# A state-space, attention and expert kernel: four attention batches issued from one written table instead of three loops

## The chip, the cores and the metric

The kernel runs on one core of a Trainium2 chip. The metric is the device time of one execution in microseconds (us), as the median of several runs. TensorE (PE) multiplies matrices and transposes, VectorE (DVE) and ScalarE (ACT) work on SBUF and PSUM, GpSimd (POOL) on SBUF alone, and SyncE (SP) issues most DMAs. Each engine takes its instructions in the order in which they were issued to it.

## The reference

Two layers act on four images of 32 x 32 positions with 256 channels. The first is a convolution with a state-space scan. The second, cut to what matters here, works on the 1024 tokens of each image:

```python
def attn(x, W_qkv, b_qkv, W_out, b_out):          # x: tokens after a layer norm
    q, k, v = split(x @ W_qkv + b_qkv, 3)
    q = q - mean(q); k = k - mean(k)              # over channels
    q2 = q * q; k2 = k * k
    k2 = l2_normalize(k2 / (sum(k2) + 1e-7), axis=tokens)
    q2 = l2_normalize(q2 / (sum(q2) + 1e-7), axis=channels)
    kv = einsum("bnc,bnd->bcd", k2, v)
    t2 = einsum("bnc,bcd->bnd", q2, kv) / sqrt(1024)
    return (v + t2) @ W_out + b_out
...
t = t + attn(layer_norm(t), ...)
t = t + ffn(layer_norm(t), ...)   # 16 experts, top 2 of a softmax gate, silu(x w1) * (x w2) w3
```

## The kernel before

The scan's stage and the experts' stage are untouched by the change. Between them stands the stage in question: attention of four batches (`b` = 0 to 3), each held as eight tiles of 128 tokens in an SBUF tile `tbs[b]`, and the routing of tokens to experts. The whole stage is issued under a manual schedule: an engine runs what it is given in the order of the Python calls, and waits are added where an instruction needs another's result or a buffer that another still uses. A new tile in a buffer waits for every use of the old one.

The stage is made of small steps, each a function of a batch and a tile, half or part:

- `stat(b, i)`: layer-norm statistics of tile i on VectorE (L1263, L1264). For the last unit of the first layer, `last_turn(j)` transposes (copied by ScalarE), `last_product(j)` multiplies by the output weights (L1301) and `last_sum` adds the result to `tbs[3]`.
- `root` and `scaled`: square root on ScalarE, reciprocal on VectorE, and then the normed tiles `xh` on ScalarE. `turn_x(b, half)`: eight transposes of `xh` (L1280), copied out by L1281.
- `qk(b, i)`: a product of 512 columns (L1336), the bias on VectorE (L1341), two squares with sums on ScalarE into `sq`, and a bias added to `tbs[b]` on POOL (L1347). `fourth(b, i)`: the sum of fourth powers on ScalarE. `k2(b, half)`: a reciprocal on VectorE (`rk`), four scalings on ScalarE (L1368), squares and folds over the tiles on POOL (L1371 to L1384).
- `v_out(b, i)`: the product of v with W_out (L1459), added to `tbs[b]` by VectorE (L1463). `turn_q(b, half)`: eight transposes of `sq` (L1280). `norm_q`, `norm_k`: the two normalizations; `norm_k` needs `fold` of POOL. `kv(b, m)`: eight products summed in PSUM (L1411), `kv_out` copies them, `kv_w` multiplies by W_out (L1442) and scales on VectorE (L1446, L1449).
- `out(b, i)`: the product with `q2T` (L1469), added into `tbs[b]` by VectorE (L1473), and the statistics of the second norm.
- `expert_in(b, half)`: normed rows `xe` on ScalarE, written to DRAM (`xd`) by SP. `turn_e`, `gates`, `turn_g`: transposes, the gate's product (L1510) and its transposes back. `route(b)`: a generator of 22 pieces, nearly all on VectorE, that finds the two experts of a token and its place in their lists. It has a product `pc` (L1569, L1570), its weights are written to DRAM by SP, POOL and ScalarE code the places, two large comparisons `qh` (L1639) follow, and a product (L1648) is added to `found`.
- `sources` turns `found` into rows to gather, `fetch_rows` gathers them by POOL, `first_weights` and `next_weights` load the first experts' weights by SP. `next_weights` puts them where `tbs[0]`, `tbs[1]` and `tbs[2]` were.

PSUM is shared by tags: `pq` has three buffers (of qk and v_out), `pt` two (transposes), `po` two (out, kv_w, norm_k, gates, turn_g, the product of route), and `pk` one (kv and `pc`). `sq`, `k2`, `ksq`, `q2T`, `xe` and `xeT` have one buffer, `xh` and `xhT` two.

Before the change three loops set the order. A first one interleaves statistics of batch 0 with the last products of the first layer, a second one issues all of qk(0, i) with statistics of batch 1, and a third one goes over `o` = 0 to 3. It issues attention of batch `o` beside qk and k2 of batch `o + 1`, statistics of `o + 2`, and gates and routing of `o - 1`, whose pieces are taken by `on_with(steps, n)` at fixed places.

Of the kernel before, what the change touches and what calls it, by code (L numbers as in the profile page):

```python
# [33 lines left out]
def conv_ssm_attn_moe_kernel(ctx: ExitStack, tc: tile.TileContext, a: dict, out: bass.AP):  # L34
# [1628 lines left out]
                break  # L1663


    for i in range(NT):
# [1 line left out]
        if i % 2 == 1:
            last_turn(i // 2)
        if i % 2 == 0 and i > 0:  # L1670
            last_product(i // 2 - 1)
        if i % HT == HT - 1:
            root(batch[0], "ln2", i + 1 - HT, i + 1)
            scaled(0, i + 1 - HT, i + 1)
    turn_x(0, 0)
    last_product(TPB - 1)
    turn_x(0, 1)
    for i in range(NT):
        qk(0, i)
        if i > 0:  # L1680
            fourth(0, i - 1)
        if i == HT:
            k2(0, 0)
        stat(batch[1], "ln2", tbs[1], i)
        if i % HT == HT - 1:
            root(batch[1], "ln2", i + 1 - HT, i + 1)
            scaled(1, i + 1 - HT, i + 1)
    fourth(0, NT - 1)
    k2(0, 1)
# [102 lines left out]
    for o in range(NB):
        n = o + 1 if o + 1 < NB else None
        z = o - 1 if o > 0 else None
        s = o + 2 if o + 2 < NB else None

        def first_part(i):
            if n is not None:
                qk(n, i)
                if i > 0:  # L1800
                    fourth(n, i - 1)

        def look_ahead(lo, hi):
            if s is not None:
                for i in range(lo, hi):
                    stat(batch[s], "ln2", tbs[s], i)

        def scale_ahead():
            if s is not None:
                root(batch[s], "ln2", 0, NT)  # L1810
                scaled(s, 0, NT)

        def turn_next(half):
            if n is not None:
                turn_x(n, half)
# [12 lines left out]
        if z is not None:
            turn_e(z, 0)
        norm_q(o)  # L1830
        if z is not None:
            root(batch[z], "ln3", HT, NT)
            expert_in(z, 1)
        turn_next(1)
        first_part(1)
        on_with(steps, 2 * pace)
        look_ahead(0, 4)
        v_out(o, 2)
        if z is not None:
            gates(z, 0)  # L1840
            turn_e(z, 1)
        else:
            for j in range(TPB):
                stat(last, "ln1", ysb, j, TPB)
            root(last, "ln1", 0, TPB)
        kv(o, 0)
        on_with(steps, 40)
        look_ahead(4, 8)
        if z is not None:
            gates(z, 1)  # L1850
        first_part(2)
        if z is not None:
            turn_g(z)
            steps = route(z)
        else:
            for j in range(TPB):
                last_sum(j)
            constants(True)
        kv(o, 1)
        on_with(steps, 2 * pace)  # L1860
        kv_out(o)
        scale_ahead()
        v_out(o, 3)
        on_with(steps, 2 * pace)
        norm_k(o)
        first_part(3)
        on_with(steps, 2 * pace)
        kv_w(o)
        if n is None:
            first_weights("w2")  # L1870
        v_out(o, 4)
        on_with(steps, 1 * pace)
        first_part(4)
        on_with(steps, 1 * pace)
        if n is not None:
            k2(n, 0)
        out(o, 0)
        on_with(steps, 1 * pace)
        out(o, 1)
        v_out(o, 5)  # L1880
        first_part(5)
        out(o, 2)
        on_with(steps, 1 * pace)
        out(o, 3)
        root(batch[o], "ln3", 0, HT)
        v_out(o, 6)
        on_with(steps, 1 * pace)
        first_part(6)
        expert_in(o, 0)
        if z is None:  # L1890
            constants(False)
        out(o, 4)
        on_with(steps, 1 * pace)
        first_part(7)
        v_out(o, 7)
        if n is not None:
            fourth(n, NT - 1)
            k2(n, 1)
        out(o, 5)
        on_with(steps, 1 * pace)  # L1900
        out(o, 6)
        on_with(steps, 1 * pace)
        if n is None:
            on_with(steps, 40)
            sources(0, SOON, found[:, 0, :SOON], found[:, 1, :SOON])
            given_rows.update(range(SOON))
            for key in soon[:3]:
                fetch_rows(key)
        out(o, 7)
        nc.scalar.dma_start(out=rows(of, o), in_=tbs[o])  # L1910
        if n is None:
            root(batch[o], "ln3", HT, NT)
            expert_in(o, 1)
            choices(0, SOON)
# [330 lines left out]
```

## Time and profile before

| | |
|---|---|
| median of 3 runs | 3376.29 us (3375.55 to 3376.74) |
| the profiled execution | 3389.96 us |
| its span, first to last instruction | 3387.8 us |
| PE busy over the span | 94% |
| DVE, ACT and POOL busy | 85%, 80% and 80% |
| first tile of `tbs[0]` landed | 2704.06 us |
| first product of kv(0, 0) | 2744.9 us |
| first product of kv(3, 0) | 2903.6 us |
| first expert product (L2008) | 2951.1 us |

Times in the profile are microseconds from the first instruction. A line of the timeline gives start, length, engine, line of the kernel, operation, the tile written and those read, shapes and the number of merged instructions. A last bracket gives the idle time of the engine ahead of it and what ended it. A matmul's record includes its way through the array, so starts are compared and not lengths. PEld is the loading of weights into TensorE, and a name with q is an engine's queue of instructions that are not counted as busy. PEclk is the granted clock of TensorE as a share of the full one.

### The profile page before, as it was taken

How to read it: one execution, taken by the hardware profiler on the slowest of the kernel's cores; microseconds unless marked ns; L12 is line 12 of the kernel's file. 1: busy time of each engine (PE TensorE's matmuls, PEld its weight loads, DVE VectorE, ACT ScalarE, POOL GpSimd, SP SyncE). 2: the span in 40 equal slices, each digit the busy share in tenths (PEclk: the TensorE clock that was granted, in tenths of full speed). 3: DMA queues.
4: the chain of work that ended last, by engine and by line, in shares of the span. 5: the costliest groups of instructions: out<-in, count | busy, mean ns of one | idle time of the engine just before them, and what ended most of it. 6: DMA issues, size and time to landing. Idle time of an engine off the chain costs nothing. (4 is left out here: it accounts for less than half of the span.)

```text
span 3387.8 us, 62750 instructions
## 1 busy us (share of the span) xinstructions
PE 3172.2 (94%) x23407; PEld 2753.3 (81%) x23407; DVE 2886.9 (85%) x3435; ACT 2717.3 (80%) x4621; POOL 2718.4 (80%) x1215
## 2 busy tenths in 40 slices
PE   7899999999999999999999999989999889789998
PEld 4588888988898888888988988768778756589998
DVE  4699999999999999999999999999999867652222
ACT  1699999999999999999999999899999754322221
POOL 0488998999999989999998999899999842234443
PEclk9999999999999999999999999999999999999999
DMA  3552224224333332253334223423222210467785
GB/s 105 150 68 63 68 66 69 71 71 62 67 78 69 68 72 76 62 63 74 73 73 68 71 64 60 71 54 68 60 62 67 80 48 29 156 186 231 214 245 149
DMA packets 423835, 300.76 MB, mean 89 GB/s; under 512 B 225073, under 2 KB 329393, under 8 KB 423522
## 3 DMA queue, kind: packets, MB, share of 16 engines
q1 hardware_dynamic: 397202, 274.25, 32.9%
q0 software_dynamic: 14016, 18.05, 2.8%
q10 hardware_dynamic: 12304, 4.37, 0.5%
q8 instruction: 187, 3.06, 0.4%
q14 instruction: 126, 1.03, 0.1%
HBM read 262.34 MB, written 34.87 MB: 88 GB/s over the span
## 5 line engine op out<-in xcount | busy, mean ns | idle before, releaser
L961 POOL TENSOR_TENSOR h<-h,cb_n 128x2048 f32<-128x2048 f32 x512 | 2154.9, 4226 | 142.6 <-DVE h L954 89.9
L928 ACT ACTIVATE da<-dt,l_conv_a_log_sb 128x512 f32<-128x512 f32 x2048 | 1438.3, 714 | 32.4 <-DVE h L954 31.3
L908 ACT ACTIVATE bx<-dtxT,proj 128x512 f32<-128x512 f32 x1748 | 1246.9, 714 | 29.9 <-DVE dtxT L600 16.4
L975 PE MATMUL y<-ident,h 128*128 128x128 f32 x8192 | 1236.5, 274 | 8.9 <-POOL h L961 5.8
L954 DVE TENSOR_TENSOR_SCAN h<-da,last,ps 128x512 f32<-128x512 f32 x1024 | 1217.9, 1262 | 7.0 <-PE ps L940 1.8
L954 DVE TENSOR_TENSOR_SCAN h<-da,ps 128x512 f32<-128x512 f32 x1024 | 1169.8, 1201 | 41.8 <-DMA last<-h 16.8
L940 PE MATMUL ps<-ident,bx 128*128 128x128 f32 x6992 | 1119.0, 276 | 41.7 <-DVE h L954 29.4
L975 PEld LDWEIGHTS y<-ident,h 128*128 128x128 f32 x8192 | 979.0, 141 | 99.9 <-issue 20.6
L940 PEld LDWEIGHTS ps<-ident,bx 128*128 128x128 f32 x6992 | 819.7, 142 | 101.8 <-DVE h L954 81.1
L2015 DVE TENSOR_TENSOR hT<-s,p 128x256 f32<-128x256 f32 x146 | 61.4, 421 | 281.0 <-ACT s L2014 281.0
L940 PE MATMUL ps<-ident,bxp 128*128 128x128 f32 x800 | 237.6, 297 | 58.9 <-DVE h L954 46.0
L2033 POOL DMA_INDIRECT out_dram<-yb,src x73 | 116.0, 1589 | 212.3 <-DVE yb L2030 82.2
L2014 ACT ACTIVATE s<-p 128x256 f32<-128x256 f32 x146 | 56.1, 384 | 265.4 <-PE p L2008 262.6
L413 PE MATMUL bg<-pad,dgc 128*128 128x256 f32 x864 | 258.2, 380 | 0.4 <-DMA dgc<-diags 0.4
L940 PEld LDWEIGHTS ps<-ident,bxp 128*128 128x128 f32 x800 | 112.3, 140 | 142.0 <-DVE h L954 89.2
L919 POOL TENSOR_SCALAR bxp<-dtxT,proj 128x512 f32<-128x512 f32 x200 | 147.0, 735 | 59.5 <-DVE dtxT L600 59.5
L935 PE MATMUL ps<-dgb,dtxT 128*128 128x128 f32 x800 | 170.3, 295 | 22.5 <-DMA dgb<-diag_b 9.7
L2008 PE MATMUL p<-xT,w 128*128 128x128 f32 x1408 | 171.7, 275 | 2.2 <-ACT xT L1988 2.2
L2008 PEld LDWEIGHTS p<-xT,w 128*128 128x128 f32 x1408 | 167.4, 192 | 5.0 <-ACT xT L1988 2.9
L935 PEld LDWEIGHTS ps<-dgb,dtxT 128*128 128x128 f32 x800 | 120.5, 190 | 49.2 <-DVE h L954 36.2
L413 PEld LDWEIGHTS bg<-pad,dgc 128*128 128x128 f32 x864 | 130.5, 191 | 0.7 <-DMA dgc<-diags 0.7
L2008 PE MATMUL p<-xT,m 128*128 128x128 f32 x928 | 115.4, 278 | 0.0
(341 smaller groups left out, 2681.6 us busy)
## 6 DMA issues: line engine op xcount, KB each, us to landing
cb_n<-cd SPq DMA_DIRECT2D x512, 256.0 KB, 3.3
m<-in_L_ffn_w_dram SPq DMA_DIRECT2D x87, 512.0 KB, 5.6
w<-in_L_ffn_w_dram SPq DMA_DIRECT2D x60, 512.0 KB, 6.9
dgc<-diags SPq DMA_DIRECT2D x84, 192.0 KB, 3.1
diag_b<-zero SPq DMA_DIRECT2D x2, 4096.0 KB
dgb<-diag_b SPq DMA_DIRECT2D x100, 64.0 KB, 3.2
last<-h SPq DMA_DIRECT2D x256, 2.0 KB, 3.1
xd<-xe SPq DMA_DIRECT2D x8, 512.0 KB, 3.5
```

Of the source, the lines that this page charges most:

```text
L413: nc.tensor.matmul(made["bg"].rearrange("p (h w) -> p h w", w=WW)[:, blk(c, deep), :], made["dgc", m * 3 + i][:, j, :], pads[m][:, at : at ...
L908: nc.scalar.activation(t, made["dtxT", u][:, j, :], AF.Copy, scale=made["proj", u][:, j, R + n : R + n + 1])
L919: nc.gpsimd.tensor_scalar(t, made["dtxT", u][:, 0, :], made["proj", u][:, 0, R + n : R + n + 1], 1.0, ALU.mult, ALU.mult,)
L928: nc.scalar.activation(t, made["dt", u][:, m, :], AF.Exp, scale=A[:, m, n : n + 1])
L935: nc.tensor.matmul(t[:, blk(j, P)], made["dtxT", steps[s][0]][:, j, blk(m, P)], made["dgb", s], start=True, stop=True,)
L940: nc.tensor.transpose(t[:, blk(j, P)], made["bx", s, j][:, blk(m, P)], ident)
L954: nc.vector.tensor_tensor_scan(h[:, m, 1:], made.pop(("da", s, m)), made.pop(("dbx", s, m)), 0.0 if seg == 0 else last[b][:, n, m : m + 1] ...
L961: nc.gpsimd.tensor_tensor(h[:, :, :BANK], h[:, :, 1:], over_middle(made["c", s], DK), ALU.mult)
L975: nc.tensor.matmul(made["y", u][j][:, blk(m, P)], made["h", s][:, m, blk(j, P)], ident, is_transpose=True, start=n == 0 and m == 0, stop=n ...
L2008: nc.tensor.matmul(p12[:, j, s, :], w_of(w, key)[:, ck, blk(h + j, P)], on_b["xT", key][:, ck, :], start=(ck == 0), stop=(ck == CK - 1),)
L2015: nc.vector.tensor_tensor(on_b["hT", key][:, h : h + 2, :], s, p12[:, :, 1, :], ALU.mult)
L2033: s = nc.gpsimd.indirect_dma_start(of[:, :], bass.IndirectOffsetOnAxis(src[:, c : c + 1], 0), yb, None, bounds_check=NB * L - 1, oob_is_er ...
```

## The change

The three loops are replaced by one tuple of steps, `ORDER`, and a dictionary that maps the short names to the same functions. The tuple has 332 entries, 69 of which (`rs`) issue one piece of a batch's route; `tg` issues the first piece too, and entries beyond the 22nd piece do nothing. Each step is there as often as before. Tiles of a batch no longer come in ascending order, and steps of up to three batches are mixed. The copy of `tbs[b]` to the output is `wr`, `first_weights` is `fw` and `next_weights` is `nw`.

```diff
-    for i in range(NT):
-        stat(batch[0], "ln2", tbs[0], i)
...
-    steps = iter(())
-    for o in range(NB):
...
-        pace = 2 if n is None else 1
-        turn_next(0)
-        if o == 3:
-            first_weights("w1")
-            first_weights("w3")
-            next_weights()
-        v_out(o, 0)
-        turn_q(o, 0)
-        v_out(o, 1)
-        turn_q(o, 1)
-        first_part(0)
...
+    def rows_in(b, half):
+        if half:
+            root(batch[b], "ln3", HT, NT)
+        expert_in(b, half)
+
+    def scale_rows(b, half):
+        lo, hi = (0, NT) if half == 2 else (half * HT, half * HT + HT)
+        root(batch[b], "ln2", lo, hi)
+        scaled(b, lo, hi)
+
...
+    STEPS = {
+        "st": lambda b, i: stat(batch[b], "ln2", tbs[b], i),
+        "sc": scale_rows, "lt": last_turn, "lp": last_product, "ll": last_stats,
+        "ls": last_sums, "co": lambda first: constants(bool(first)), "tx": turn_x, "qk": qk,
+        "f4": fourth, "k2": k2, "vo": v_out, "tq": turn_q, "nq": norm_q, "kv": kv,
+        "ko": kv_out, "nk": norm_k, "kw": kv_w, "ou": out,
+        "r3": lambda b: root(batch[b], "ln3", 0, HT), "ei": rows_in, "te": turn_e,
+        "ga": gates, "tg": begin_route, "rs": lambda b: next(routes[b], None),
+        "fw": first_weights, "nw": next_weights, "so": first_lists, "wr": put_rows_out,
+        "ch": lambda: choices(0, SOON),
+    }
+    ORDER = (
+        ('st', 0, 0), ('st', 0, 6), ('lt', 0), ('lt', 1), ('st', 0, 5), ('st', 0, 2), ('lp', 0),
+        ('lt', 2), ('st', 0, 1), ('st', 0, 3), ('sc', 0, 0), ('st', 0, 4), ('st', 0, 7),
+        ('st', 1, 0), ('st', 1, 1), ('lp', 1), ('st', 1, 4), ('lt', 3), ('lp', 2), ('tx', 0, 0),
+        ('lp', 3), ('sc', 0, 1), ('qk', 0, 0), ('st', 1, 2), ('tx', 0, 1), ('st', 1, 3),
+        ('sc', 1, 0), ('qk', 0, 2), ('st', 1, 5), ('qk', 0, 5), ('qk', 0, 1), ('qk', 0, 3),
+        ('f4', 0, 5), ('f4', 0, 0), ('st', 1, 6), ('qk', 0, 4), ('st', 1, 7), ('vo', 0, 0),
+        ('f4', 0, 2), ('f4', 0, 4), ('vo', 0, 4), ('k2', 0, 0), ('qk', 0, 6), ('tx', 1, 0),
+        ('sc', 1, 1), ('f4', 0, 1), ('qk', 0, 7), ('vo', 0, 1), ('f4', 0, 7), ('tq', 0, 0),
+        ('f4', 0, 3), ('st', 2, 0), ('f4', 0, 6), ('k2', 0, 1), ('st', 2, 5), ('qk', 1, 0),
+        ('st', 2, 1), ('st', 2, 7), ('qk', 1, 1), ('tq', 0, 1), ('qk', 1, 2), ('f4', 1, 2),
+        ('vo', 0, 2), ('st', 2, 2), ('ll',), ('tx', 1, 1), ('f4', 1, 0), ('kv', 0, 0),
+        ('vo', 0, 7), ('st', 2, 6), ('qk', 1, 3), ('qk', 1, 4), ('vo', 0, 5), ('st', 2, 3),
+        ('nq', 0), ('st', 2, 4), ('qk', 1, 5), ('kv', 0, 1), ('ls',), ('ko', 0), ('nk', 0),
+        ('k2', 1, 0), ('kw', 0), ('co', 1), ('vo', 1, 1), ('sc', 2, 2), ('vo', 0, 6),
+        ('ou', 0, 0), ('ou', 0, 1), ('vo', 0, 3), ('f4', 1, 1), ('ou', 0, 2), ('tx', 2, 0),
+        ('qk', 1, 6), ('ou', 0, 3), ('f4', 1, 4), ('ou', 0, 6), ('vo', 1, 0), ('r3', 0),
+        ('ei', 0, 0), ('ou', 0, 4), ('f4', 1, 5), ('qk', 1, 7), ('st', 3, 0), ('f4', 1, 6),
+        ('ou', 0, 7), ('k2', 1, 1), ('st', 3, 5), ('tq', 1, 0), ('ou', 0, 5), ('kv', 1, 0),
+        ('f4', 1, 3), ('tq', 1, 1), ('wr', 0), ('f4', 1, 7), ('nq', 1), ('ei', 0, 1),
+        ('qk', 2, 0), ('tx', 2, 1), ('vo', 1, 2), ('te', 0, 0), ('qk', 2, 1), ('st', 3, 1),
+        ('te', 0, 1), ('st', 3, 2), ('f4', 2, 0), ('co', 0), ('st', 3, 6), ('ga', 0, 0),
+        ('ga', 0, 1), ('st', 3, 4), ('vo', 1, 3), ('nk', 1), ('tg', 0), ('st', 3, 7), ('rs', 0),
+        ('qk', 2, 2), ('kv', 1, 1), ('rs', 0), ('st', 3, 3), ('rs', 0), ('ko', 1), ('sc', 3, 2),
+        ('rs', 0), ('vo', 1, 6), ('qk', 2, 3), ('f4', 2, 2), ('rs', 0), ('rs', 0), ('kw', 1),
+        ('qk', 2, 4), ('f4', 2, 1), ('vo', 1, 4), ('rs', 0), ('ou', 1, 0), ('k2', 2, 0),
+        ('rs', 0), ('f4', 2, 3), ('ou', 1, 2), ('qk', 2, 6), ('rs', 0), ('rs', 0), ('rs', 0),
+        ('ou', 1, 3), ('ou', 1, 4), ('vo', 2, 1), ('qk', 2, 5), ('ou', 1, 1), ('qk', 2, 7),
+        ('vo', 1, 7), ('r3', 1), ('ei', 1, 0), ('k2', 2, 1), ('vo', 1, 5), ('f4', 2, 5),
+        ('tx', 3, 0), ('rs', 0), ('ou', 1, 5), ('ou', 1, 7), ('rs', 0), ('vo', 2, 0), ('rs', 0),
+        ('f4', 2, 4), ('vo', 2, 2), ('f4', 2, 7), ('rs', 0), ('te', 1, 0), ('kv', 2, 0),
+        ('tq', 2, 0), ('rs', 0), ('ou', 1, 6), ('f4', 2, 6), ('qk', 3, 0), ('qk', 3, 1),
+        ('tq', 2, 1), ('ei', 1, 1), ('vo', 2, 7), ('qk', 3, 2), ('ga', 1, 0), ('te', 1, 1),
+        ('rs', 0), ('rs', 0), ('rs', 0), ('rs', 0), ('rs', 0), ('ga', 1, 1), ('tx', 3, 1),
+        ('tg', 1), ('vo', 2, 4), ('rs', 1), ('rs', 1), ('rs', 0), ('rs', 1), ('wr', 1),
+        ('kv', 2, 1), ('f4', 3, 0), ('rs', 1), ('ko', 2), ('nq', 2), ('nk', 2), ('rs', 1),
+        ('qk', 3, 5), ('rs', 1), ('f4', 3, 1), ('rs', 1), ('kw', 2), ('qk', 3, 3), ('f4', 3, 3),
+        ('ou', 2, 0), ('vo', 2, 3), ('rs', 1), ('ou', 2, 4), ('qk', 3, 4), ('rs', 1),
+        ('ou', 2, 1), ('k2', 3, 0), ('f4', 3, 4), ('ou', 2, 3), ('ou', 2, 2), ('rs', 1),
+        ('r3', 2), ('qk', 3, 7), ('rs', 1), ('rs', 0), ('ei', 2, 0), ('vo', 2, 5), ('qk', 3, 6),
+        ('rs', 1), ('ou', 2, 7), ('vo', 2, 6), ('ou', 2, 5), ('te', 2, 0), ('ou', 2, 6),
+        ('f4', 3, 7), ('tq', 3, 0), ('ei', 2, 1), ('ga', 2, 0), ('rs', 1), ('vo', 3, 1),
+        ('tq', 3, 1), ('f4', 3, 6), ('fw', 'w3'), ('rs', 1), ('vo', 3, 0), ('te', 2, 1),
+        ('f4', 3, 2), ('k2', 3, 1), ('rs', 1), ('f4', 3, 5), ('rs', 1), ('rs', 1), ('vo', 3, 2),
+        ('nq', 3), ('rs', 1), ('ga', 2, 1), ('kv', 3, 0), ('tg', 2), ('rs', 1), ('rs', 2),
+        ('rs', 2), ('rs', 2), ('rs', 2), ('kv', 3, 1), ('nw',), ('ko', 3), ('wr', 2), ('rs', 2),
+        ('rs', 2), ('rs', 2), ('rs', 2), ('nk', 3), ('fw', 'w2'), ('vo', 3, 4), ('rs', 2),
+        ('rs', 2), ('kw', 3), ('vo', 3, 3), ('rs', 2), ('rs', 2), ('rs', 2), ('ou', 3, 0),
+        ('rs', 2), ('rs', 1), ('rs', 1), ('rs', 2), ('rs', 2), ('ou', 3, 1), ('ou', 3, 3),
+        ('rs', 2), ('ou', 3, 2), ('rs', 2), ('r3', 3), ('vo', 3, 5), ('rs', 2), ('ei', 3, 0),
+        ('ou', 3, 4), ('vo', 3, 6), ('rs', 2), ('rs', 2), ('rs', 1), ('so',), ('vo', 3, 7),
+        ('ou', 3, 6), ('fw', 'w1'), ('rs', 2), ('rs', 1), ('ou', 3, 5), ('ou', 3, 7), ('wr', 3),
+        ('ei', 3, 1), ('rs', 2), ('ch',),
+    )
+    for name, *at in ORDER:
+        STEPS[name](*at)
```

More of the change, by code (lines that the diff above doesn't have):

```diff
@@ L1663, in on_with @@
                 break
-    for i in range(NT):
-        stat(batch[0], "ln2", tbs[0], i)
[L1668 to L1689, printed above, removed]
     late = ex
@@ L1789, in fetch_rows @@
         on_b["xb", key] = t
-    steps = iter(())
-    for o in range(NB):
[L1793 to L1815, printed above, removed]
-        pace = 2 if n is None else 1
-        turn_next(0)
-        if o == 3:
-            first_weights("w1")
-            first_weights("w3")
-            next_weights()
-        v_out(o, 0)
-        turn_q(o, 0)
-        v_out(o, 1)
-        turn_q(o, 1)
-        first_part(0)
[L1828 to L1914, printed above, removed]
@@ new lines, in rows_in, with begin_route, last_stats @@
+    def rows_in(b, half):
[6 more added lines that the diff above has]
+        scaled(b, lo, hi)
+    routes = {}
+    def begin_route(b):
+        turn_g(b)
+        routes[b] = route(b)
+        next(routes[b])
+    def last_stats():
+        for j in range(TPB):
+            stat(last, "ln1", ysb, j, TPB)
+        root(last, "ln1", 0, TPB)
@@ new lines, in last_sums, with first_lists, put_rows_out @@
+    def last_sums():
+        for j in range(TPB):
+            last_sum(j)
+    def first_lists():
+        for b in routes:
+            for _ in routes[b]:
+                pass
+        sources(0, SOON, found[:, 0, :SOON], found[:, 1, :SOON])
+        given_rows.update(range(SOON))
+        for key in soon[:3]:
+            fetch_rows(key)
+    def put_rows_out(b):
+        nc.scalar.dma_start(out=rows(of, b), in_=tbs[b])
+    STEPS = {
[9 more added lines that the diff above has]
+    }
```

## The prediction

> **What bounds the kernel now.** I first read the windows of 20 us, to find the stage that the table orders. It begins when the last scan products leave TensorE, at 2698 us, and ends with the first expert matmul at 2951 us. The windows show which engine could be the limit:
>
> ```profile
> core 0: us, PE busy (x) PEld busy (x) DVE busy (x) ACT busy (x) POOL busy (x), PEclk, DMA share, GB/s
> 2720.00:2740.00 20.00, 16.09 (x56) 9.66 (x55) 12.89 (x34) 16.09 (x62) 8.59 (x8) 0.91 0.00 1
> ...
> 2800.00:2820.00 20.00, 19.37 (x79) 12.80 (x78) 11.38 (x39) 12.12 (x35) 0.00 (x0) 1.00 0.00 1
> 2820.00:2840.00 20.00, 15.45 (x60) 11.07 (x59) 17.35 (x46) 8.67 (x31) 10.74 (x9) 0.91 0.13 36
> ...
> 2920.00:2940.00 20.00, 16.80 (x71) 13.44 (x70) 16.46 (x45) 3.49 (x7) 1.47 (x1) 0.75 0.14 32
> ```
>
> No engine is full throughout. TensorE is near it at 2800 to 2820 us, VectorE at 2820 to 2840 us, and in the last row neither is, at a granted clock of 0.75. So order can matter. Next I read the timeline of TensorE, which shows where its time goes and what each idle stretch waited for (the last bracket):
>
> ```profile
> 2730.51 1.03 PE L1459 MATMUL pv<-wvs,xhT 128*128 128x256 f32 x4
> 2735.45 1.97 PE L1280 MATMUL ps_t<-ident,sq 128*128 128x128 f32 x8 [3.91 <-DVE xhT L1281]
> ...
> 2828.76 1.89 PE L1469 MATMUL po<-kvw,q2T 128*128 128x256 f32 x8
> 2833.82 1.59 PE L1469 MATMUL po<-kvw,q2T 128*128 128x256 f32 x4 [3.16 <-DVE tb L1473]
> ...
> 2868.71 1.89 PE L1442 MATMUL pkw<-wvs,kvT 128*128 128x256 f32 x8
> ...
> 2919.34 0.46 PE L1569 MATMUL pc<-hot,every_t 128*128 128x128 f32 x2 [3.29 <-DVE both L1572]
> 2919.64 0.59 PE L1570 MATMUL pc<-hot,before_t 128*128 128x128 f32 x2
> 2920.03 3.41 PE L1442 MATMUL pkw<-wvs,kvT 128*128 128x256 f32 x8
> ```
>
> Starts to starts on this timeline give the price of each step at full clock: qk 1.71 us (four records), vo and ou 0.86, kv 3.45, kw 1.73, lp 1.73, ga 1.75, tx, tq, te and nk about 0.87, tg 0.6. Times their counts, and with route's three products, they make 191 us. From 2699.4 us to the last `out` at 2940.9 us pass 241.5 us, so some 50 us are lost. About 38 are the bracketed gaps; the rest is slow matmul after a gap: the same eight pkw took 3.41 us behind a gap of 3.29, and 1.89 without one. Cut at the starts of kv(b,0), the losses are: up to kv(0,0) at 2744.9, 45.5 us for 33.5 of work, 12.0 lost; to kv(1,0) at 2796.0, 51.1 for 43.9, 7.2; to kv(2,0) at 2853.1, 57.1 for 46.7, 10.4; to kv(3,0) at 2903.6, 50.4 for 42.3, 8.1; to the last `out`, 37.4 for 25.0, 12.4.
>
> **The change part by part.** No instruction is added or removed: the steps are the same, and route's 22 pieces of each batch are all issued before first_lists. So only gaps can go or come. Behind the last `out` the order is unchanged (root, expert_in, turn_e, gates, then the first rows); those 10.2 us stay, and I price the experts' stage at nothing, if weights and rows are there in time (below).
>
> *Up to kv(0,0).* Both halves of tb0 are issued together; the first landed at 2704.06, and at 350 GB/s, which the DMA moved there, 512 KB more take 1.5 us. stat(0,6) now stands second and waits for that, so scaled(0,0) comes 2 us later. But in the old order the third last_turn's copy stood on ScalarE behind the four xh, and TensorE got to turn_x(0,0) at 2711.9 only. Now copies 0 to 2 precede the xh, and TensorE does its lp without holes: turn_x at 2709.5, qk(0,0) at 2712.9, turn_x(0,1) done at 2715.5, with 12.1 us of its work behind it. Before, it had 10.4 at 2715.9. That is 2.1 us. Then the gap of 3.91: ScalarE was busy from 2718.5 to 2737.7 with squares, xh of batch 1 and k2, and TensorE had run out. Now vo(0,0), vo(0,4), vo(0,1), tq(0,0) and qk(1,0) stand there, 5.2 us. The gap goes, and the slow matmuls behind it (ps_t 1.97 where 1.04 is usual, pv 1.80 for 1.03). 3.9 + 1.7 = 5.6. Together **7.7 us**. What is late next is ScalarE on sq(1,0): `sq` has one buffer, and tq(0,1) that frees it stands behind qk(1,1). It waits some 2 us, with k2(0,1) already done, and TensorE holds other work. If not covered, half of the 5.6 comes back.
>
> *kv(0,0) to kv(1,0).* Gaps of 1.63 (pkn behind the last sums), 1.38 (pkw) and some of 0.5. In the new order nk(0) alone lies between kv(0,1) and kw(0), where vo and qk stood, so kv_out (0.69 us) shows for 0.2; but vo(1,1) and vo(0,6) cover the two kvw. Then 13.7 us of TensorE against 14.9 of VectorE up to kv(1,0). I leave 3.7 of the 7.2 lost: **3.5 us** gained (bounds 0 and 5).
>
> *kv(1,0) to kv(3,0).* Of 18.5 lost, the worst places are runs of `out` at the end of a batch. VectorE needs 1.06 us for one (0.48 + 0.43 + 0.18, part of it overlapped), TensorE 0.86, and into that run fell the pieces of route and k2's rk, which waited 1.57 for squares just issued. Now vo(1,7), vo(1,5), turn_x(3,0) and later te(1,0) and kv(2,0) lie among them, and k2(3,1) follows its last qk by 20 steps. New waits: the evictions of tq(1,0) and tq(2,0) write the one q2T, and must wait for out(0,5) and out(1,6), which stand behind them on TensorE; sq(3,0) waits on ScalarE for tq(2,1), with gates' copy queued behind; route(0)'s five last pieces come in a row, so its product waits for two qh. 9 of the gaps can go (2833 with its slow matmuls 5, and 2890, 2896 for 4), the four waits cost 0 to 2.5 each, and I take 5 for all: **4 us** gained (bounds -1 and 9).
>
> *kv(3,0) to the last `out`.* gates(2,1), a qh and the product of route(1) leave the stretch between kv(3,0) and pc: 15.8 us for 11.7 of TensorE become about 11.5 for 9.2, 4 less. From pc on VectorE sets the pace, 24.1 us then and, with the same steps, now. Against it: `pf` of route(1) is taken 25 steps before it is used and holds one of two `po` buffers over nk(3), kw(3) and out(3,0), 1 us (0 to 3); fold(3) needs 8.4 us of POOL behind k2(3,1) and nk(3) comes 11 us of work later, 1 us (0 to 3). The third is VectorE against POOL. In POOL's timeline:
>
> ```profile
> 2835.59 1.89 POOL L1371 TENSOR_TENSOR ksq<-k 128x1024 f32<-128x1024 f32 x1 [8.45 <-ACT k L1368]
> ```
>
> VectorE's timeline around it, with the same operation twice:
>
> ```profile
> 2834.36 0.36 DVE L1604 TENSOR_TENSOR pick<-hot_all,run 128x128 f32<-128x128 f32 x1
> ...
> 2836.03 1.70 DVE L1604 TENSOR_TENSOR pick<-hot_all,run 128x128 f32<-128x128 f32 x1
> ```
>
> The same pick took 0.36 us alone and 1.70 when it began inside ksq, ending 0.25 us after it. The new order puts route(1)'s two qh (1.19 to 2.38 us) and route(2)'s first pieces beside the fold of k2(3,1), where POOL had been idle from 2905 to 2928. Two qh at 1.2 more and three picks or the like at 0 to 1.34 are 2.4 to 6.4; I take 4, near the middle; as such pieces were caught elsewhere before, at half that, 2 remain. The Trainium skill (SBUF — State Buffer, "Who interferes with whom") has the rule: a VectorE instruction with two SBUF inputs and a POOL instruction that reads SBUF exclude each other for a whole instruction. The trace agrees: the pick ended just after ksq. By the rule alone, an estimate with seven small ones each held for half of a 1.27 us fold would be 6.8 us where I took 4, and the forecast 3 us less gain.
>
> Sum here **0 us** (4 - 1 - 1 - 2; bounds -8 and 4).
>
> *The queue of SP.* next_weights now stands ahead of the copy out of tb2, whose place its third load takes:
>
> ```profile
> 2889.01 1.49 SPq L1773 DMA_DIRECT2D w<-in_L_ffn_w_dram  x2
> 2890.55 14.33 SPq L1753 DMA_DIRECT2D m<-in_L_ffn_w_dram  x6
> 2904.92 0.51 SPq L1494 DMA_DIRECT2D xd<-xe  x1
> ```
>
> SP held there for 14.33 us, 9.3 of them for such a copy, with xe's write queued behind. Now w2, route(2)'s weights and xe of batch 3 are behind it. It is free some 16 us after kv(3,1), 11 us behind pc, and the rows are gathered 22 us behind pc. w1, issued last, lands (6.9 us) 5 us before the first expert matmul. Cost nothing; without that cover, a us for each us.
>
> The sum: 7.7 + 3.5 + 4 + 0 = 15.2 us. The profiled execution took 3389.96 us (span 3387.8), 0.4% over the median of 3376.29; on the median the forecast is 3361, in a profile about 3375.
>
> **The rivals.**
> *Slower: steps ahead of what frees their buffer.* Five places (tq(1,0), tq(2,0), qk(3,0), pf, fold(3)) are priced small above. If each opens a TensorE gap like the 3.16, with 1.9 of slow matmuls behind it, they cost 25.5 us instead of 7, and the 15.2 become 3 lost; with POOL's collisions at their bound, 4.4 more, 3384. It decides from four such gaps. For it: gaps of 3 us did come from one late VectorE instruction. Against: in each place TensorE has 1 to 4 us of other work. Chance 0.2.
> *Only the beginning gains.* VectorE is busy 16 to 17 of 20 us in late windows, and `po` has two buffers whatever the order. The later gaps would move and not close: 8 us, 3368. The Trainium skill (Perfetto Trace Analysis, "Optimization Strategy") reads the same gap, repeated, as too few buffers, which speaks against any order; the trace shows 11 waits of po on L1473, but not evenly spaced. Chance 0.15.
> *Nearly full TensorE.* If only 20 of 50 us stay, 3346. For it, 2744 to 2828 ran with 7 lost of 84. Chance 0.12.
> *Given back.* Weights or rows come late and the experts begin when they did: 3376. Chance 0.06.
>
> **How the numbers follow.** The forecast has 0.47, by itself 3352 to 3370. A measurement of this kernel can tell about 0.2%, 6.8 us. The main case, the full one and half of the second are faster by more: 0.67. The other half and the last are within: 0.13. Slower 0.20. The range reaches from 3345, the full case, to 3382, which leaves out the worst half of the slower rival.
>
> **What would show it.** In the changed profile: the kv(0,0) products (L1411) 5 us earlier; no gap of 3 us before it; L1569 of batch 2 some 12 us after the last kv(3,0) began; a span from L1469's last to L2008's first of 10 us. I am wrong if TensorE gaps behind L1281 or L1473 add up to as much as before, or if L2008 waits for w or xb.

## The result, and the profile after

| | before | after |
|---|---|---|
| median | 3375.92 us (3375.08 to 3376.74, 4 runs) | 3352.47 us (3347.83 to 3355.56, 4 runs) |
| profiled execution | 3389.96 us, span 3387.8 | 3350.39 us, span 3348.6 |
| the stage, first last_turn to first expert product | 251.8 us | 226.6 us |
| experts' stage | 436.7 us | 438.7 us |

The kernel became faster by 23.45 us: the ratio is 0.9929 (95% interval 0.9916 to 0.9941). The two profiled executions differ by more, 39.6 us, because the scan's stage, with the same instructions in both, ended 16.1 us earlier in one than in the other (first last_turn at 2699.4 and 2683.3). So everything below is counted from the start of the stage. There 25.2 us were gained, and the experts gave back 2.0.

The windows of the changed kernel, cut at the starts of kv(b,0) and at the last `out`:

```profile
core 0: us, PE busy (x) PEld busy (x) DVE busy (x) ACT busy (x) POOL busy (x), PEclk, DMA share, GB/s
2682.50:2723.80 41.30, 37.66 (x157) 24.23 (x158) 26.39 (x74) 28.81 (x97) 13.79 (x15) 1.00 0.42 132
2723.80:2755.90 32.10, 32.10 (x143) 24.66 (x142) 26.53 (x77) 15.13 (x55) 18.87 (x28) 1.00 0.03 10
2755.90:2808.45 52.55, 49.52 (x214) 34.04 (x212) 41.49 (x120) 29.93 (x91) 19.37 (x19) 0.97 0.14 45
2808.45:2865.60 57.15, 56.11 (x259) 36.92 (x257) 49.84 (x126) 30.56 (x92) 19.46 (x19) 1.00 0.17 50
2865.60:2901.20 35.60, 27.72 (x145) 22.62 (x144) 32.17 (x86) 8.53 (x18) 12.14 (x9) 0.86 0.48 153
```

The second row is new: TensorE is busy for 32.10 of 32.10 us, with no gap at all. The fourth is near it. The fifth is still the place that loses, and there VectorE is the busiest. TensorE's timeline, at the places that were shown of before:

```profile
2714.28 1.03 PE L1459 MATMUL pv<-wvs,xhT 128*128 128x256 f32 x4
2715.15 1.04 PE L1280 MATMUL ps_t<-ident,sq 128*128 128x128 f32 x8
...
2797.14 1.13 PE L1469 MATMUL po<-kvw,q2T 128*128 128x256 f32 x4 [2.30 <-DVE tb L1473]
2798.11 3.19 PE L1336 MATMUL pqk<-wqk,xhT 128*128 128x512 f32 x4
...
2875.39 0.61 PE L1427 MATMUL pkn<-ones,fold 128*128 128x1 f32 x4 [1.51 <-POOL fold L1384]
2880.85 0.77 PE L1569 MATMUL pc<-hot,every_t 128*128 128x128 f32 x2 [3.88 <-DVE nk L1433]
```

The gap of 3.91 us ahead of tq(0,0) is gone (the ps_t<-ident,sq at 2715.15 follows its pv at once, and takes 1.04 and not 1.97). One large gap is left in the middle, of 2.30 us behind L1473, and the qk behind it takes 3.19 us for a usual 1.88. In all, TensorE's waits for L1473 went from 9.6 to 4.3 us, and those for VectorE's L1281 from 8.7 to 0.7. Ahead of pc the gap did not shrink: 3.29 then, 3.88 now. Why shows on VectorE:

```profile
2865.76 1.86 DVE L1395 TENSOR_SCALAR low<-sums 128x8 f32<-128x8 f32 x1
2867.72 1.24 DVE L1396 TENSOR_TENSOR rq<-rq,low 128x8 f32<-128x8 f32 x1
2868.99 0.20 DVE L1397 RECIPROCAL rq<-rq 128x8 f32<-128x8 f32 x1
2869.11 2.24 DVE L1639 TENSOR_TENSOR qh<-places,qb 128x1024 bf16<-128x1024 bf16 x1
...
2871.91 1.42 DVE L1529 TENSOR_TENSOR pr<-pr,m 128x128 f32<-128x128 f32 x1
```

and on POOL in the same microseconds:

```profile
2865.70 1.89 POOL L1371 TENSOR_TENSOR ksq<-k 128x1024 f32<-128x1024 f32 x1 [11.56 <-ACT k L1368]
2867.67 2.60 POOL L1383 TENSOR_TENSOR two<-two,ksq 128x512 f32<-128x512 f32 x2
2870.35 1.60 POOL L1384 TENSOR_TENSOR fold<-two 128x256 f32<-128x256 f32 x1
```

`low` is an operation on eight numbers of each partition that took 0.16 to 0.23 us elsewhere in this trace; here it took 1.86, and ended 0.03 us after ksq. SP's queue was held by the loads behind the copy out of tb2:

```profile
2862.76 17.05 SPq L1727 DMA_DIRECT2D m<-in_L_ffn_w_dram  x6
```

It was free at 2879.81, 1 us ahead of pc, where the prediction had it 11 us behind.

### The profile page after: what moved, and what is told of

It reads as the page before. It is cut to its first block, busy times and chain, and to the rows that moved or that the text cites. A ratio compares the mean times of both kernels' runs of the same rounds, so it can differ in the third digit from the quotient of the medians.

```text
span 3348.6 us, 62734 instructions
## 1 busy us (share of the span) xinstructions
PE 3163.7 (94%) x23407; PEld 2752.2 (82%) x23407; DVE 2891.9 (86%) x3435; ACT 2717.2 (81%) x4621; POOL 2717.1 (81%) x1215
## 3 DMA queue, kind: packets, MB, share of 16 engines
q1 hardware_dynamic: 397202, 274.25, 31.8%
## 5 line engine op out<-in xcount | busy, mean ns | idle before, releaser
L954 DVE TENSOR_TENSOR_SCAN h<-da,ps 128x512 f32<-128x512 f32 x1024 | 1169.4, 1200 | 30.3 <-ACT da L928 13.1
L940 PE MATMUL ps<-ident,bxp 128*128 128x128 f32 x800 | 236.7, 296 | 50.2 <-DVE h L954 37.3
L935 PE MATMUL ps<-dgb,dtxT 128*128 128x128 f32 x800 | 171.3, 296 | 21.6 <-DMA dgb<-diag_b 10.7
L1958 PE MATMUL p<-xT,w 128*128 128x128 f32 x1408 | 173.4, 277 | 2.2 <-ACT xT L1938 2.2
L1958 PEld LDWEIGHTS p<-xT,w 128*128 128x128 f32 x1408 | 169.1, 193 | 5.2 <-ACT xT L1938 3.0
L1958 PE MATMUL p<-xT,m 128*128 128x128 f32 x928 | 115.3, 278 | 0.0
```

Source lines behind the costliest of these rows:

```text
L935: nc.tensor.matmul(t[:, blk(j, P)], made["dtxT", steps[s][0]][:, j, blk(m, P)], made["dgb", s], start=True, stop=True,)
L940: nc.tensor.transpose(t[:, blk(j, P)], made["bx", s, j][:, blk(m, P)], ident)
L954: nc.vector.tensor_tensor_scan(h[:, m, 1:], made.pop(("da", s, m)), made.pop(("dbx", s, m)), 0.0 if seg == 0 else last[b][:, n, m : m + 1] ...
L1958: nc.tensor.matmul(p12[:, j, s, :], w_of(w, key)[:, ck, blk(h + j, P)], on_b["xT", key][:, ck, :], start=(ck == 0), stop=(ck == CK - 1),)
```

## The experiments

Each row is one profiled execution, its stage cut in the same places (us between the starts; the last column is the sum). Runs 1 to 4, 5 to 8 and 9 to 12 were on three chips, on which the kernel before took 3377.37, 3384.77 and 3386.70 us, so kernels are compared by their ratio to it.

| | to kv(0,0) | kv(1,0) | kv(2,0) | kv(3,0) | last out | first product | stage |
|---|---|---|---|---|---|---|---|
| before | 45.5 | 51.1 | 57.1 | 50.4 | 37.0 | 10.6 | 251.8 |
| after | 40.5 | 32.1 | 52.6 | 57.1 | 35.5 | 8.8 | 226.6 |
| 1 new front | 40.4 | 48.7 | 58.0 | 50.9 | 37.0 | 10.6 | 245.5 |
| 2 old front | 49.7 | 32.6 | 50.2 | 58.0 | 36.6 | 10.0 | 237.1 |
| 3 old end | 42.1 | 32.1 | 50.2 | 58.0 | 44.3 | 10.9 | 237.6 |
| 4 fold earlier | 42.1 | 32.1 | 50.2 | 60.2 | 34.7 | 9.5 | 228.8 |
| 5 both | 40.9 | 32.1 | 50.2 | 60.2 | 35.7 | 10.9 | 230.0 |
| 6 no fold | 40.5 | 32.1 | 50.2 | 58.0 | 30.2 | 10.0 | 221.0 |
| 7 ScalarE copies | 42.7 | 32.1 | 53.1 | 57.7 | 35.2 | 10.0 | 230.8 |
| 8 old order, out in pq | 45.6 | 51.8 | 58.7 | 51.3 | 37.0 | 10.6 | 255.0 |
| 9 buffers mended | 40.6 | 32.1 | 50.2 | 62.2 | 36.2 | 10.0 | 231.3 |
| 10 fold between | 40.4 | 32.1 | 50.2 | 59.6 | 34.5 | 10.0 | 226.9 |
| 11 the same, squares on ScalarE | 42.3 | 32.1 | 50.9 | 60.8 | 30.8 | 10.0 | 226.9 |
| 12 after again | 41.0 | 32.1 | 50.2 | 58.0 | 37.1 | 9.6 | 227.9 |

My theory was that each part of the table closes gaps of its own stretch, by order alone. The rivals were that only the beginning gains, that gaps come from too few buffers, and that the table's early steps cost a gap at each buffer.

**1. The table up to kv(0,0), then the old order.**

```diff
         ('vo', 0, 2), ('st', 2, 2), ('ll',), ('tx', 1, 1), ('f4', 1, 0), ('kv', 0, 0),
-        ('vo', 0, 7), ('st', 2, 6), ('qk', 1, 3), ...        # the changed table
+        # what is left of the steps, as the three loops had them
```

> The new table up to its kv(0,0), then all other steps in the old order. The two profiles, cut at the kv(b,0), give 7.5 us to this stretch (5.0 us earlier with 2.6 us more of TensorE's work done). If each stretch gains by its own steps, this kernel gains those 7.5 us and no more: 3368 us, and the stretch from kv(0,0) to kv(1,0) still loses about 7 us against its work. If the second stretch lost only because ScalarE and POOL came late out of the first one, its 6.9 us go here too: 3361. If the parts only work together, it is within 2 us of 3376.

3371.60 us (3367.76 to 3374.21), ratio 0.9984 (0.9974 to 0.9993): 5.8 us faster, where 7.7 was my term. The first stretch is the changed kernel's, 40.4 us, and the second still loses 7.4 (48.7 for 41.3 of TensorE's work). So the beginning gains alone, and what follows does not gain because of it.

**2. The reverse: the old order up to kv(0,0), then the table.**

```diff
-        ('st', 0, 0), ('st', 0, 6), ('lt', 0), ('lt', 1), ...
+        ('st', 0, 0), ('st', 0, 1), ('lt', 0), ('st', 0, 2), ...   # the two first loops, and o = 0 up to kv(0,0)
```

> The converse: the old order up to kv(0,0), the table behind it. By stretches that gain by their own steps: 23.5 less 7.5 is 16 us gained, 3360, and the gap of 3.9 us ahead of the first tq(0,0) is back. If the second stretch's loss is carried over from the first: 9 us gained, 3367.

3363.03 us (3360.38 to 3363.37), ratio 0.9955 (0.9939 to 0.9972): 14.3 us faster. With the 5.8 of the first that is 20.1 of 23.5, which the intervals allow. The rival "only the beginning gains" falls: it left nothing for this kernel. TensorE's timeline has the gap ahead of tq(0,0) again, and eight lp matmuls at half their rate (granted clock 0.53):

```profile
2695.11 3.62 PE L1301 MATMUL po_l<-l_conv_w_out_sb,yT 128*128 128x256 f32 x8 [2.37 <-ACT yT L1294]
...
2722.58 1.96 PE L1280 MATMUL ps_t<-ident,sq 128*128 128x128 f32 x8 [3.88 <-DVE xhT L1281]
```

This stretch took 49.7 us where it took 45.5 in the profile of before, but it holds one qk and one v_out more, so that the steps behind it are the table's: 2.6 us of work. So 13.6 us are lost here, and 12.0 were before. Slow lp are in both, in other places: in the profile of before it is the first lp that took 3.40 us, behind a gap of 0.80.

**3. The table up to kv(3,0), then the old end.**

```diff
-        ('nq', 3), ('rs', 1), ('ga', 2, 1), ('kv', 3, 0), ('tg', 2), ('rs', 1), ('rs', 2),
+        ('nq', 3), ('rs', 1), ('ga', 2, 1), ('wr', 2), ('fw', 'w1'), ('nw',), ('kv', 3, 0),
+        ('rs', 1), ('rs', 1), ('rs', 1), ('tn', 2), ...   # route(1)'s last pieces at once
+        # tn is tg without the first piece of the route
```

> The new table up to kv(3,0), the old order from there (next_weights, w1 and the copy out of tb2 ahead of kv(3,0)). The stretch from kv(3,0) to the last out lost 12.4 us against its work in both profiles, so by the cuts the old end costs nothing: 3353, with 2 us to either side for the 1.7 us by which the new end starts the experts sooner behind the last out. If the new end did gain, and paid it back for POOL's folds that stand beside it (they stay where they are here), it is slower by 4: 3357.

3362.60 us (3361.29 to 3366.73), ratio 0.9955 (0.9939 to 0.9972), 9 to 10 us worse than I expected. I had called the end worth nothing. The first product of route(1) stood on TensorE and waited:

```profile
2883.24 1.44 PE L1648 MATMUL pf_r<-code,qh 128*128 128x96 bf16 x16 [7.49 <-POOL code L1628]
```

while POOL had the squares and folds of k2(3,1) ahead of that code:

```profile
2872.15 1.89 POOL L1371 TENSOR_TENSOR ksq<-k 128x1024 f32<-128x1024 f32 x1 [11.55 <-ACT k L1368]
...
2881.03 0.72 POOL L1384 TENSOR_TENSOR fold<-two 128x256 f32<-128x256 f32 x1
2881.71 1.47 POOL L1628 TENSOR_TENSOR code<-code,groups 128x768 bf16<-128x768 bf16 x1
```

So the table can have its late k2(3,1) because its last pieces of route(1) are late too: `pf`, held for 25 steps, which I priced as a loss, is one of the steps that keep TensorE from standing behind POOL. The two belong together.

**4. The table with k2(3,1) 13 steps earlier.**

```diff
-        ('f4', 3, 7), ('tq', 3, 0), ('ei', 2, 1), ...  ('f4', 3, 2), ('k2', 3, 1), ('rs', 1),
+        ('f4', 3, 7), ('k2', 3, 1), ('tq', 3, 0), ('ei', 2, 1), ...  ('f4', 3, 2), ('rs', 1),
```

> The new table with k2(3,1) moved 13 steps forward, behind fourth(3,7). In the changed profile VectorE's small operations beside its folds took 6.4 us longer than alone (low 1.86 for 0.18, rq 1.24 for 0.17, qh 2.24 for 1.19, two route operations 1.42 and 1.14 for 0.29), pkn waited 1.5 us for fold and pc 3.9 us for VectorE. If the folds are what holds the end, pc comes 4 to 5 us sooner behind kv(3,0) and the time is 3348. If the collisions only move to the steps ahead of kv(3,0), it is 3352, with the same 6 us found there.

3349.75 us (3347.32 to 3354.62), ratio 0.9916 (0.9900 to 0.9933), which overlaps the changed kernel's interval. pc comes 13.0 us after kv(3,0) began, and 15.3 in the changed kernel, but the stretch ahead is longer (60.2 for 57.1 to 58.0), with a new wait in TensorE's timeline:

```profile
2866.27 1.24 PE L1280 MATMUL ps_t<-ident,xe 128*128 128x128 f32 x8 [1.82 <-ACT xe L1490]
```

ScalarE itself waited there for VectorE, whose operation ahead of xe ran beside POOL's squares:

```profile
2863.02 1.55 DVE L1486 SCALAR_TENSOR_TENSOR nm<-ln_mv,ln_rs 128x4 f32<-128x4 f32 x1
```

In the changed kernel the median of this operation is 0.16 us. The loss mostly moved: the four scalings stand ahead of the square root that nm needs, and nm meets the squares.

**5. Both: that table up to kv(3,0), and the old end** (one run).

> The new table up to kv(3,0) with k2(3,1) 13 steps sooner, then the old order. With the old end behind the late k2(3,1), the product of route(1) waited 7.5 us on POOL, whose place coding stands behind the fold. If that conflict is all that made the old end slower, the wait shrinks to 2 us or less, the stretch from kv(3,0) takes 38 us where it took 44.3, and the stage (first last_turn to first expert product) comes to 230 us. If the new end is better by itself, the stretch stays at 41 or more.

3359.40 us; the last stretch took 35.7 us, where the old end behind the late fold took 44.3. Its stage, 230.0 us, is near the 228.8 of run 4. So the 7.49 us of run 3 came from the order of fold and code on POOL, and the old end as such costs little.

**6. Without the fold.** Of batch 3's second half POOL makes neither squares nor four of its sums, so norm_k(3) is of half the tokens and the routing comes out otherwise. More expert blocks run then, and only the stage can be read (one run, 3586.97 us).

```diff
+        few = b == NB - 1 and half == 1
+        if not few:
             nc.gpsimd.tensor_tensor(on["ksq"][:, lo:hi, :], ...)
...
-                for i in (lo, lo + 2):
+                for i in () if few else (lo, lo + 2):
```

> The new table; POOL leaves out the squares and the four adds of batch 3's second half, so norm_k(3) sees half of the tokens. POOL's run beside the end of route(1) and the start of route(2) falls from 8.6 to 1.5 us. If VectorE's long small operations there come from POOL (low 1.86, rq 1.24, a pr 1.42, a cand 1.14), they return to 0.2 to 0.3, and pc comes about 5 us sooner behind kv(3,0), 10 us where it was 15.3. If they are long for another reason, nothing moves.

The last stretch fell from 35.5 (37.1 in run 12) to 30.2 us, pc stood 11.4 us after kv(3,0), and VectorE's timeline has the same operations at other prices:

```profile
2874.83 1.10 DVE L1397 TENSOR_SCALAR low<-sums 128x8 f32<-128x8 f32 x1
2876.24 0.17 DVE L1398 TENSOR_TENSOR rq<-rq,low 128x8 f32<-128x8 f32 x1 [0.31 <-ACT rq L1395]
...
2876.57 1.17 DVE L1641 TENSOR_TENSOR qh<-places,qb 128x1024 bf16<-128x1024 bf16 x1
...
2879.64 0.29 DVE L1531 TENSOR_TENSOR pr<-pr,m 128x128 f32<-128x128 f32 x1
```

Against after: 0.76 for low, 1.07 for rq, 1.07 for qh and 1.13 for pr; with the copy `rest` (0.71 for 0.23) and `cand` (1.14 for 0.29) that is 5.4 us of VectorE's time (`cand` stood beside POOL's `code`, which the fold holds back). Not all of it reached pc, 3.9 us sooner: VectorE now waits 1.26 us for the gates' transposes. Most of the rest lies behind pc, where kw, no longer behind so long a gap, took 1.89 us for 2.90. The wait of pkn for `fold`, 1.51 us, goes with the fold too, but pc stood behind VectorE, by its bracket. So POOL's fold beside VectorE is what the last stretch pays.

**7. Half of the copies of turn_x and turn_q, and kv_out(3), on ScalarE.**

```diff
-        turned(..., batch[b]["q2T"], half, (nc.vector.tensor_copy,) * 2)
+        turned(..., batch[b]["q2T"], half, on_both)
```

> The new table; of the two copies of each turn_x and turn_q the first goes to ScalarE (as it did for turn_x of batch 0 alone), and kv_out of batch 3 too. ScalarE is busy 30 of 57 us ahead of kv(3,0), VectorE 50. If VectorE holds the second half, it loses 0.63 us at 14 places and 0.7 at one, about 9 us, and a third to a half of that shows: 3349. If ScalarE's queue is the tighter one at these places (copies behind squares, squares behind copies), it is 3355 to 3360.

3365.44 us (3363.71 to 3367.56), ratio 0.9939 (0.9922 to 0.9955), not distinguishable from the changed kernel's. No gain: by the windows VectorE is busy for 49.84 of 57.15 us in the fourth stretch, and freeing it did not bring TensorE, busy for 56.11 there, through sooner: 57.7 us.

**8. The old order, with `out` in the three buffers of pq.**

```diff
-        po = ps_c.tile([P, C], F32, name="po1", tag="po")
+        po = ps_b.tile([P, C], F32, name="po1", tag="pq", bufs=3)
```

> The old order, with out's product in the three buffers that qk and v_out use, so that it no longer shares two with kv_w, norm_k and gates. If the idle stretches of TensorE at out come from too few buffers, the 21.5 us of waits of L1469 on L1473 shrink by half and the time is 3366. If they come from VectorE's order, the waits only move to the same place on another tag and the time stays within 4 us of 3376.

3386.56 us (3381.84 to 3390.70), ratio 1.0007 (0.9997 to 1.0016): nothing. The waits of TensorE and its weight loads in the stage (us in total, times, longest), of before:

```profile
PEld po L1469 <- DVE tb L1473: 11.9, 6, 3.6
PE po L1469 <- DVE tb L1473: 9.6, 5, 3.2
PEld ps_t L1280 <- DVE xhT L1281: 7.3, 5, 4.3
PE ps_t L1280 <- DVE xhT L1281: 5.8, 3, 3.9
```

and of this kernel:

```profile
PEld ps_t L1280 <- DVE xhT L1281: 11.6, 5, 5.2
PE ps_t L1280 <- DVE xhT L1281: 10.0, 3, 4.8
PEld po L1469 <- DVE tb L1473: 7.5, 6, 2.0
PE po L1469 <- DVE tb L1473: 4.3, 4, 1.6
```

The waits for L1473 halve (21.5 to 11.8, weight loads and matmuls together), and those for L1281 grow by nearly as much (13.1 to 21.6). The Trainium skill (Perfetto Trace Analysis, "Optimization Strategy") reads a gap that repeats as possibly too few buffers; here three buffers in place of two gained nothing, and another order made the stage 25 us shorter. The three are shared with qk and v_out, so buffers changed their users and a larger number in all was not tried.

**9. The table, with the steps I had priced as early put right.**

```diff
-        ('ou', 0, 7), ('k2', 1, 1), ('st', 3, 5), ('tq', 1, 0), ('ou', 0, 5), ('kv', 1, 0),
+        ('ou', 0, 7), ('k2', 1, 1), ('st', 3, 5), ('ou', 0, 5), ('tq', 1, 0), ('kv', 1, 0),
-        ('tq', 2, 0), ('rs', 0), ('ou', 1, 6), ('f4', 2, 6), ('qk', 3, 0), ('qk', 3, 1),
-        ('tq', 2, 1), ('ei', 1, 1), ...
+        ('rs', 0), ('ou', 1, 6), ('tq', 2, 0), ('f4', 2, 6), ('tq', 2, 1), ('qk', 3, 0),
+        ('qk', 3, 1), ('ei', 1, 1), ...
-        ... ('kv', 3, 0), ('tg', 2), ('rs', 1), ('rs', 2),
+        ... ('kv', 3, 0), ('tg', 2), ('rs', 2), ...    # and this piece of route(1) next to its following one
```

> The changed table with the four buffer places that I had priced put right: tq(1,0) issued behind out(0,5), tq(2,0) behind out(1,6), tq(2,1) ahead of qk(3,0), and route(1)'s 20th piece, which takes pf, directly ahead of its 21st. The rival (steps ahead of what frees their buffer cost a TensorE gap of 3 us and slow matmuls each): at least 5 us shorter than the changed kernel, stage below 222 us. My sum (each place 0 to 2.5 us, covered by other TensorE work): within 2 us of the changed kernel, stage 225 to 229, kv(1,0) to kv(3,0) 107 to 110 us where the change has 109.7.

3362.74 us (3361.86 to 3366.44), ratio 0.9935 (0.9920 to 0.9950). It is no faster, and its stage is 3.4 us longer than that of run 12 on the same chip. What was mended opened a gap where there had been none:

```profile
2822.19 1.39 PE L1280 MATMUL ps_t<-ident,sq 128*128 128x128 f32 x8 [3.84 <-DVE q2T L1281]
2823.38 5.20 PE L1336 MATMUL pqk<-wqk,xhT 128*128 128x512 f32 x8
```

The second tq now follows the first on TensorE and waits for VectorE's copies of `q2T`, and the two qk behind it take 5.20 us for a usual 3.60. The price of one gap in my slower rival (3.2 and 1.9 of slow matmuls) is about right: 3.84 and 1.6. The table has no such gap there, with two qk between the two halves. At the other places that this run put right nothing changed: the stretches of tq(1,0) took 32.1 and 50.2 us as in run 12, and that of `pf` 36.2, for 35.5 and 37.1 in the two profiles of the table.

**10 and 11. The fold between.** k2(3,1) directly behind expert_in(2,1); in run 11 ScalarE makes its squares as well.

```diff
-        ('f4', 3, 7), ('tq', 3, 0), ('ei', 2, 1), ('ga', 2, 0), ('rs', 1), ('vo', 3, 1),
+        ('f4', 3, 7), ('rs', 1), ('tq', 3, 0), ('ei', 2, 1), ('k2', 3, 1), ('ga', 2, 0),
...   # and k2(3, 1) goes from its old place
# run 11 only, in k2(3, 1), in place of POOL's ksq:
+            for i in range(lo, hi):
+                nc.scalar.activation(on["ksq"][:, i, :], on["k2"][:, i, :], AF.Square)
```

> The changed table, with k2(3,1) issued directly behind expert_in(2,1), earlier than in the last kernel that moved it, and route(1)'s 14th piece ahead of tq(3,0). POOL's fold then runs beside VectorE's turns and biases, which read PSUM, and not beside gates(2,1) and the first comparison of route(2). Theory (VectorE beside POOL's fold is the loss behind kv(3,0)): that stretch 31 to 33 us where the change has 35.5, nothing lost ahead of it, stage 222 to 224, a median 3 us below the changed kernel's. Rival (the collisions only move, as the last kernel that moved the fold showed): the stretch to kv(3,0) longer by what the last one is shorter, median within 1.5 us of the changed kernel's. Second rival (ScalarE's four scalings of k2 now stand ahead of the second half's xe and copies): 2 us slower.

> As the one before, and the squares of k2(3,1) are made by ScalarE in four instructions, where POOL made them in one of 1.89 us; nothing is left out. If POOL's work beside VectorE is what costs: 1 to 2 us below the one before. If ScalarE's queue is the tighter one: four squares of about 0.45 us stand ahead of its copies and it is 1 to 2 us above.

3361.56 us (3354.53 to 3365.90), ratio 0.9927 (0.9914 to 0.9941), and 3359.45 us (3356.37 to 3363.75), ratio 0.9925 (0.9911 to 0.9938), beside 0.9925 for the unchanged table in run 12. The last stretch shrank (34.5 and 30.8 us, for 35.5 and 37.1 in the two profiles of the table), to the 31 to 33 of the theory in run 11 alone, and the one ahead grew (59.6 and 60.8 for 57.1 and 58.0). In run 11 TensorE waits for the copy of xeT ahead of gates(2,1), which stands on ScalarE behind the four scalings (1.69 us) and the four squares (1.32):

```profile
2876.49 1.89 PE L1514 MATMUL pgT<-xeT,l_ffn_gate_w_sb 128*16 128x512 f32 x4 [2.53 <-ACT xeT L1281]
```

Over the two stretches run 11 has 91.6 us and run 12 95.1, but its other stretches gave back 2.4 and the medians do not differ. No version here beats the table by more than these runs can tell.

**12. The changed kernel again.**

> The changed kernel once more, beside the three above on one chip: 3352 within 5 us, stage 226.6 within 2 us, first stretch 40.4 to 42.7 us. If the half-rate matmuls fall in other places from one execution to the next, the stretches differ by 2 us with the same steps, and differences of that size between kernels show nothing.

3361.43 us (3358.30 to 3364.40), ratio 0.9925 (0.9910 to 0.9940). The level is the chip's: the kernel before took 3386.70 on it. The ratio stands. The third stretch, 52.6 us in the first profile, is 50.2 here, with the same instructions. On TensorE's timeline the gap of 2.30 is 1.63 now, and the qk behind it is fast:

```profile
2808.02 1.13 PE L1469 MATMUL po<-kvw,q2T 128*128 128x256 f32 x4 [1.63 <-DVE tb L1473]
2808.99 1.88 PE L1336 MATMUL pqk<-wqk,xhT 128*128 128x512 f32 x4
```

VectorE had `wts`, two small products beside POOL's fold of k2(2,0), in 1.15 us where the first profile has 2.32:

```profile
2804.59 1.15 DVE L1575 TENSOR_TENSOR wts<-m,both 128x8 f32<-128x8 f32 x2
```

Runs 2 to 5, 9 and 10 have the same steps there, and agree with this one: `wts` in 1.15 to 1.17 us, a gap of 1.60 to 1.64, a stretch of 50.2. Run 11 has wts at 2.33 and the gap at 2.30 as in the first profile, but the qk behind it at the full rate, and 50.9 us:

```profile
2807.87 1.13 PE L1473 MATMUL po<-kvw,q2T 128*128 128x256 f32 x4 [2.30 <-DVE tb L1477]
2808.84 1.88 PE L1336 MATMUL pqk<-wqk,xhT 128*128 128x512 f32 x4
```

So differences of 2 us between two stretches of single profiles show nothing of the order of steps, and I rest no verdict on one.

## Why the prediction was right, step by step

The direction and its reason held: no instruction changed, TensorE's lost time went from 49.7 us of these stretches to 26.4, and the kernel is faster. By windows cut at these starts, 17.2 of the 23.3 were idle time of TensorE (32.0 us, then 14.8) and 6.2 were slow matmuls (busy for 209.2, then 203.0, with the same work). The prediction had put about 38 of its 50 us into gaps, and its last stretch ran to 2940.9, where the last matmul of `out` began at 2940.6: 37.0 us, 12.0 lost. In all 23.45 us were gained where my sum had 15.2, and two terms had the wrong size, a third the wrong parts. By lost time (a stretch less TensorE's work in it, from the starts of the timeline):

- **Up to kv(0,0): 7.7 forecast, 7.6 measured** (12.0 lost, then 40.5 us for 36.1 of work, 4.4). The gap ahead of tq(0,0) went and no wait for sq(1,0) took its place. Of what is still lost, 2.2 us are a gap ahead of turn_x(0,0), which waits for `xh` of ScalarE. Run 1 gained 5.8 with this part alone.
- **kv(0,0) to kv(1,0): 3.5 forecast, bounds 0 and 5; 6.9 measured.** Work of 31.8 us took 32.1. The step that failed is "I leave 3.7 of the 7.2 lost". I had set 13.7 us of TensorE against 14.9 of VectorE in one part of the stretch and made a loss of it; over the whole stretch VectorE had 26.53 of 32.10 us, and TensorE held other batches' products to run ahead with. Run 2 keeps this gain (32.6) without the new front, so it belongs to these steps.
- **kv(1,0) to kv(3,0): 4 forecast, bounds -1 and 9; 9.1 measured** (18.5 lost, then 109.7 us for 100.3, 9.4; 10.6 gained by run 12). The gaps I had named went, and that was my 9; the four waits for which I took off 5 cost almost nothing. In the changed trace none of them shows as a gap of over 0.4 us (in run 12 the product of route(0) waits 0.88 for its qh), and run 9, which takes the early steps away, gains nothing by it, though at tq(2,0) its own new gap hides what the early place cost. I had given a price to each step that stands ahead of what frees its buffer, without asking in each place what TensorE holds next.
- **kv(3,0) to the last `out`: 0 forecast, 0.3 lost.** The sum is right and its terms are not. To pc it was to be 11.5 us; it is 15.3, before 15.8. Of the 4 us that I counted as gain, 2.5 were TensorE's work (11.7 less 9.2) that the table does ahead of kv(3,0), where it lengthens that stretch: a move, not a gain. And POOL against VectorE costs 5.4 us (run 6), where I halved 4 to 2. Behind pc 1.7 us less were lost. "pf, 1 us" was no loss: run 9 took it away and the stretch stayed, and in run 3 the end without it was the slower one.
- **POOL against VectorE by the rule.** In the trace TENSOR_SCALAR, TENSOR_TENSOR and a COPY stretch beside the fold, while RECIPROCAL keeps 0.20 us and TENSOR_REDUCE 0.29; low, `rest` and cand ended 0.03 to 0.15 us after the POOL instruction that they began beside. The Trainium skill (SBUF — State Buffer, "Who interferes with whom") has that a VectorE instruction that needs the ports it shares with POOL and a POOL instruction exclude each other for a whole instruction, reductions excepted. The trace agrees; my estimate by it, 6.8 us, was nearer to the 5.4 than my 2.
- **The tail, unchanged at 10.2 forecast: 10.6 then, 8.8 after, 9.6 in run 12. The experts, nothing forecast: 436.7 us, then 438.7.** The two cancel: from the last `out` to the end of the span 447.2 and 447.5 us passed. In the profile of before the last product of the gates took 3.42 us at a granted clock of 0.53, and the first 16 products of the experts 2.05 at 1.00; after, the gates took 2.34 at 0.79 and the products (L1958) 3.78 at 0.50. In run 12, with the changed table too, it is the gates again (3.31, and 2.05 for the products). So the slow matmuls fall into one of the two stretches or the other, with the same order. Rows and weights were not late: w1 was issued at 2899.58, and none of these products waits for a DMA.

So the stretches up to the last `out` gained 23.3 us, and the medians differ by 23.45. Of the prediction's signs, kv(0,0) came 5.0 us earlier and the waits for L1281 and L1473 fell; pc of batch 2 stood 15.3 us behind kv(3,0), where 12 were forecast.

Of the rivals, the slower one fell to the timeline and to run 9, "only the beginning gains" to run 2, and "given back" to the experts' 2.0 us. "Nearly full TensorE" was nearer in time than the forecast, 3346, yet not in its picture: the beginning, kv(1,0) to kv(3,0) and the end still lose 4.4, 9.4 and 12.3 us. The prediction's "11 waits of po on L1473" were six places, with weight loads and matmuls counted apart. That the whole gain is more than the sum of runs 1 and 2, 20.1 for 23.5, lies within the intervals; whether old and new steps that meet at kv(0,0) cost something is open. So is what decides where matmuls go at half rate.

## What to carry to other kernels

Count lost time, not time, when steps move between stretches: work that goes elsewhere is no gain. Before you charge a step for standing ahead of what frees its buffer, look at what its engine's queue holds in between; here such steps cost next to nothing, and one put right cost a gap of 3.84 us with slow matmuls behind it. When an end of a schedule looks free, look for the pair that carries it: here it was late pieces of routing with a late fold on POOL.
